# A Strassen MLP inside two attention blocks: two weight groups per step on the way down, operands written after each product, weight differences on GpSimd, and other staging tiles

## The chip, the cores and the metric

The kernel runs on one core of a Trainium2 chip. The time is device microseconds of one execution. Each core has TensorE (PE, matrix products into PSUM), VectorE (DVE), ScalarE (ACT), GpSimd (POOL) and SyncE (SP, whose queue issues all the DMAs here). Matrix products read SBUF and write the eight PSUM banks; DMAs move tiles between DRAM and SBUF.

## The reference

Sixteen sequences of 256 tokens with 512 channels go through two blocks. Block 0 is cross-attention with a mask and a residual, followed by an MLP (layer norm, 512 to 2048 channels, exact gelu, back to 512, residual). Block 1 is self-attention, cross-attention and a small MLP. The change is in the MLP of block 0 (and in what lies just before and after it):

```python
x = x + out
h = layer_norm(x, n2_w, n2_b)
h = jax.nn.gelu(h @ fc1_w + fc1_b, approximate=False) @ fc2_w + fc2_b
return x + h
```

All is float32. Products are made in three passes: an operand is split into a rounded high part and the low rest, and high x high, high x low and low x high are added up in PSUM. A split is one cast on ScalarE (the high part) and one subtract (the low part).

## The kernel before

The tokens are worked in groups of 512 (two sequences), eight groups in all. The kernel has three parts in time: phase 1 (attention of block 0, a stream of heads into which projections are woven), the MLP of block 0 (`Mlp0`), and block 1. TensorE's instructions run in the order in which the program writes them (`manual_schedule`). The instructions of the other engines and of SP are put in order by the framework, by its own estimate of when each is due; each engine then runs its list in order, so an instruction that waits holds up all those behind it. Tiles come from pools; a tile with one buffer can be filled again only when the last reader of its former content is done.

`Mlp0` uses one level of Strassen's scheme in Winograd's form: a product of two 2x2 block matrices takes seven block products instead of eight, from operands that are blocks, sums and differences of blocks (`differences` makes four of them: s1 = a21 + a22, s2 = s1 - a11, s3 = a11 - a21, s4 = a12 - s2). `OPS` says which operand of the tokens and which of the weights belongs to each product.

*The weights.* They are cut into eight groups of 256 hidden channels. `weigh(way, m)` loads a raw group (512 KB, tile `wst`), makes four differences (two on GpSimd, L821 and L822, two on VectorE, L823 and L824) and splits seven blocks into the tiles `w_h` and `w_l` (`split_lazy`, L141 on ScalarE and L142 on VectorE). Way 1 is fc1, way 2 is fc2, which is put into the same tiles when the way up is done with them.

*The way up.* A group of tokens takes four steps of two weight groups each (`up`, 84 products of 128x256 a step). Its seven operands lie in the slots `x_t` and `c_t`, split from the transposed normalized tokens; those of the next group are written (`operand_up`) in the last step, each after the product that last reads its slot. `turn` transposes a tile of 128 tokens (L843) for the next group, with four evictions by ScalarE for even tiles and by VectorE for odd ones (L847). The tile `ho` collects a step's hidden values, which go to DRAM (`hid`, 1 MB a step).

*The way down.* A group of tokens takes eight steps of one weight group each, 42 products a step. For each step the hidden values are loaded (`hidden`, 512 KB, two steps ahead), the sums made (`sums_down`, L789 and L790 on GpSimd, L791 and L792 on VectorE) and seven operands split into one of two sets of slots, both one step ahead:

```python
            for n in range(total):
                ...
                if n + 1 < total:
                    self.sums_down(n + 1)
                    self.operands_down(n + 1)
                ...
                for i in (1, 6, 2, 7, 5, 4, 3):
                    if n or i not in (1, 6):
                        self.product_down(n, i)
                    if m == self.NM - 1:
                        self.end(g, i, xs[g])
```

The seven products of a group (L991) add up over its steps in seven PSUM banks. In the last step `end` adds each of them to the residual tile `x`: seven sums that read PSUM on VectorE (L1021 to L1036) and four on GpSimd (L1022, L1023, L1028, L1029). A product of the next group can start in its bank when those sums have read it. `residual` loads the four tiles of x and adds the bias on GpSimd (L1004).

*The edges.* The end of phase 1 (`last`) splits the first two weight groups, normalizes, turns and writes the first group's operands between the last heads; the other six groups are split in `run`, ahead of its first step. In the last group of the way up, `weigh(2, ...)` follows the steps that free its tiles. At the end `front` loads and transposes the first tokens of block 1 between the last products.

Of the kernel before, what the change touches and what calls it, by code (L numbers as in the profile page):

```python
# [41 lines left out]
def kernel(ctx: ExitStack, tc: tile.TileContext, a, out):  # L42
# [96 lines left out]
    def split_lazy(src, h, l):  # L139

        nc.scalar.copy(h, src)  # L141
        nc.vector.tensor_tensor(l, src, h.bitcast(F32), ALU.subtract)  # L142
# [87 lines left out]
    def ln_stats(pool, src):  # L230

        st = pool.tile([P, nc.vector.BN_STATS_DIM], F32, tag="bnst", name="st")
        mv = pool.tile([P, nc.vector.BN_AGGR_DIM], F32, tag="bnmv", name="mv", bufs=4)
        nc.vector.bn_stats(st, src)
        nc.vector.bn_aggr(mv, st)
        rstd = pool.tile([P, 2], F32, tag="bnrs", name="rstd", bufs=4)
        nc.vector.tensor_scalar(rstd[:, 0:1], mv[:, 1:2], EPS, None, ALU.add)  # L237
        nc.gpsimd.tensor_tensor(out=rstd[:, 1:2], in0=rstd[:, 0:1], in1=nhalf, op=ALU.pow)  # L238
        return mv[:, 0:1], rstd[:, 1:2]

    def normalize(pool, dst, src):
        mean, rstd = ln_stats(pool, src)
# [308 lines left out]
    def phase1():  # L551
# [173 lines left out]
        def last():  # L725
            yield from more_values(NG - 1)
            right.close()
            mlp = w["mlp"] = Mlp0()
            yield from residual(NG - 2, 1)
            for m in range(mlp.EARLY):  # L730
                mlp.weigh(1, m)
                yield 12 * PASS
            yield from residual(NG - 1, 0)
            for t in range(G):
                yield mlp.turn(0, t, mlp.normal(0, t, pool, "xr"))
            mlp.sums()
            for i in range(mlp.NP):
                mlp.operand_up(i)
# [10 lines left out]
    class Mlp0:  # L749
# [13 lines left out]
        NP = 7  # L763
        EARLY = 2
# [5 lines left out]
        def __init__(self):  # L770
# [5 lines left out]
            self.w, self.wp, self.raw, self.banks = {}, {}, {}, {}  # L776

            tiles = pair(self.ins, "x_t") + pair(self.ins, "c_t")
            self.slots = [t[:, i, :] for t in tiles for i in range(KC)]
# [3 lines left out]
            ]  # L783


        def differences(self, a21, a22, a11, a12, out):

            s1, s2, s3, s4 = out
            nc.gpsimd.tensor_tensor(out=s1, in0=a21, in1=a22, op=ALU.add)  # L789
            nc.gpsimd.tensor_tensor(out=s3, in0=a11, in1=a21, op=ALU.subtract)  # L790
            nc.vector.tensor_tensor(s2, s1, a11, ALU.subtract)  # L791
            nc.vector.tensor_tensor(s4, a12, s2, ALU.subtract)  # L792

        def weigh(self, way, m):


            raw = self.pool.tile([P, 4 * 2 * P], F32, tag="wst", name="raw", bufs=3)
            if way == 1:
                src = a["fc1_w"][:, ts(m, 2 * P)].rearrange("(k p) c -> p k c", p=P)
                view = raw.rearrange("p (k c) -> p k c", k=KC)  # L800
                nc.sync.dma_start(out=view, in_=src)
                b = [[view[:, 2 * k : 2 * k + 2, ts(n, P)] for n in range(2)] for k in range(2)]
            else:
                src = a["fc2_w"][ts(m, 2 * P), :].rearrange("(k p) c -> p k c", p=P)
                view = raw.rearrange("p (k c) -> p k c", k=2)
                nc.sync.dma_start(out=view, in_=src)
                b = [[view[:, k, ts(n, 2 * P)] for n in range(2)] for k in range(2)]
            if m not in self.w or way == 2:
                if way == 1:
                    self.wp[m] = sbuf(self.stack, f"w{m}", 1, "right")  # L810
                self.w[m] = tuple(
                    self.wp[m].tile([P, self.NP, 2 * P], F32R, tag=f"w{x}", name=f"w{m}_{x}")
                    for x in "hl"
                )
            diff = self.pool.tile([P, 4, 2 * P], F32, tag="wst", name="diff", bufs=3)

            def like(x):
                return x.rearrange("p (k c) -> p k c", k=2) if way == 1 else x

            t1, t2, t3, t4 = (like(diff[:, i, :]) for i in range(4))  # L820
            nc.gpsimd.tensor_tensor(out=t1, in0=b[0][1], in1=b[0][0], op=ALU.subtract)  # L821
            nc.gpsimd.tensor_tensor(out=t3, in0=b[1][1], in1=b[0][1], op=ALU.subtract)  # L822
            nc.vector.tensor_tensor(t2, b[1][1], t1, ALU.subtract)  # L823
            nc.vector.tensor_tensor(t4, b[1][0], t2, ALU.subtract)  # L824
            h, l = self.w[m]
            for i, x in enumerate((b[0][0], b[1][0], b[1][1])):
                split_lazy(x, like(h[:, i, :]), like(l[:, i, :]))
            split_lazy(diff, h[:, 3:, :], l[:, 3:, :])


        def normal(self, g, t, pool, tag="xn"):
            x = pool.tile([P, C], F32, tag=tag, name="xn")
            nc.sync.dma_start(out=x, in_=xd[0][g][ts(t, P), :])
            normalize(pool, x, x)
            return x

        def turn(self, g, t, x):
# [6 lines left out]
            for c in range(KC):  # L844
                to, gain, offset = self.x[:, c, ts(t, P)], n2[:, 0, c : c + 1], n2[:, 1, c : c + 1]
                if t % 2:
# [5 lines left out]
        def sums(self):  # L852
# [5 lines left out]
            self.differences(b[1][0], b[1][1], b[0][0], b[0][1], [s[:, i] for i in range(4)])  # L858
            self.a = [b[0][0], b[0][1], b[1][1]] + [s[:, i] for i in range(4)]

        def up_slots(self, i):
            return [
                self.slots[8 * x + i].rearrange("p (k n) -> p k n", n=self.W) for x in range(2)
            ]

        def operand_up(self, i):
            split_lazy(self.a[i], *self.up_slots(i))

        def product_up(self, n, i, tag, first):
            g, s = divmod(n, self.NS)  # L870
            ao, bo = self.OPS[i]
            x = self.up_slots(ao)
# [15 lines left out]
            if s == self.NS - 1 and g + 1 < NG:  # L888
# [576 lines left out]
```

## Time and profile before

| what | us |
|---|---|
| median of three runs (2858.71 to 2864.98) | 2864.82 |
| the profiled execution | 2866.24 |
| its span, first to last instruction | 2864.5 |
| TensorE busy | 2700.0 (94%) |
| VectorE busy | 2087.5 (73%) |
| ScalarE busy | 1855.6 (65%) |
| GpSimd busy | 894.9 (31%) |
| first and last product of the way up | 725.8, 1081.1 |
| first and last product of the way down | 1073.8, 1479.0 |

A row of a timeline has the start, the length, the engine, the line, the operation, what it writes and reads, and in brackets how long the engine had been idle before it and who ended that. A row of the waits has who waited for whom, the microseconds in total, how often, and the longest. The TensorE's mean granted clock is 0.974 of full speed.

### The profile page before, as it was taken

How to read it: one execution, taken by the hardware profiler on the slowest of the kernel's cores; microseconds unless marked ns; L12 is line 12 of the kernel's file. 1: busy time of each engine (PE TensorE's matmuls, PEld its weight loads, DVE VectorE, ACT ScalarE, POOL GpSimd, SP SyncE). 2: the span in 40 equal slices, each digit the busy share in tenths (PEclk: the TensorE clock that was granted, in tenths of full speed). 3: DMA queues.
4: the chain of work that ended last, by engine and by line, in shares of the span. 5: the costliest groups of instructions: out<-in, count | busy, mean ns of one | idle time of the engine just before them, and what ended most of it. 6: DMA issues, size and time to landing. Idle time of an engine off the chain costs nothing.

```text
span 2864.5 us, 57571 instructions
## 1 busy us (share of the span) xinstructions
PE 2700.0 (94%) x18970; PEld 2270.2 (79%) x18970; DVE 2087.5 (73%) x6129; ACT 1855.6 (65%) x5504; POOL 894.9 (31%) x960
## 2 busy tenths in 40 slices
PE   7999999997999997898989999999999999999998
PEld 5777777775899986898978777777777777777787
DVE  6676666757865678898977777777777677776887
ACT  4877777777554554444437777777777777787632
POOL 6122221212210115555441222224433233233533
PEclk9999999998999998999999999999999999999999
DMA  7566565554333353434355565566665555555321
GB/s 226 171 195 179 170 179 168 185 169 127 133 130 118 122 183 121 143 124 143 123 191 190 182 189 178 182 186 210 205 192 174 178 181 179 171 177 170 97 100 59
DMA packets 292282, 465.47 MB, mean 162 GB/s; under 512 B 36753, under 2 KB 188817, under 8 KB 287889
## 3 DMA queue, kind: packets, MB, share of 16 engines
q1 hardware_dynamic: 291984, 461.79, 51.2%
q8 instruction: 153, 2.51, 0.4%
q14 instruction: 145, 1.18, 0.1%
HBM read 284.97 MB, written 176.69 MB: 161 GB/s over the span
## 4 chain that ended last, share of the span: by engine, by line
PE 70%; DVE 11%; DMA 9%; ACT 5%; issue 3%; SPq 1%; POOL 1%; POOLq 0%; DVEq 0%; ACTq 0%
PE ps_v L259 15%; PE ps_p L259 14%; PE down L991 10%; PE ps_pt L450 8%; PE ps_z L466 5%; PE ps_s L409 5%; PE up_sc L880 4%; PE up_pt L880 3%; DMA d<-qk 3%; PE up_mm L880 3%; ACT e L434 2%; PE ps_t L278 2%; DMA x<-xd 2%; DVE e L424 1%; DVE c_t L142 1%
## 5 line engine op out<-in xcount | busy, mean ns | idle before, releaser
L434 ACT ACTIVATE e<-e,mn 128x256 f32<-128x256 f32 (+1 forms) x1024 | 487.7, 480 | 86.6 <-DVE mn L424 85.5
L453 ACT COPY pt<-ps_pt 128x512 f32<-128x512 f32 (+1 forms) x768 | 421.4, 554 | 142.0 <-PE ps_pt L450 135.0
L450 PE MATMUL ps_pt<-ident,e 128*128 128x128 f32 x2816 | 439.5, 275 | 13.5 <-ACT pt L453 12.8
L450 PEld LDWEIGHTS ps_pt<-ident,e 128*128 128x128 f32 x2816 | 338.2, 141 | 56.5 <-ACT pt L453 20.0
L409 PE MATMUL ps_s<-stack 97*128 97x256 f32 (+1 forms) x1536 | 334.5, 299 | 28.8 <-ACT e L434 22.0
L409 PEld LDWEIGHTS ps_s<-stack 97*128 97x128 f32 (+1 forms) x1536 | 268.9, 191 | 93.7 <-ACT e L434 39.1
L434 ACT ACTIVATE e<-ps_s,mn 128x256 f32<-128x256 f32 x512 | 244.4, 496 | 65.6 <-DVE mn L420 60.2
L1219 POOL TENSOR_TENSOR x<-x,zz 128x256 f32<-128x256 f32 x128 | 95.2, 744 | 609.7 <-DVE zz L1212 577.3
L238 POOL TENSOR_TENSOR rstd<-rstd,nhalf 128x1 f32<-128x1 f32 x192 | 127.3, 669 | 484.1 <-DVE rstd L237 436.9
L424 DVE CUSTOM_DVE_ANT_0 e<-mb,ps_s 128x256 f32<-128x256 bf16 x512 | 192.6, 415 | 77.9 <-PE ps_s L409 75.2
L991 PE MATMUL down<-w_h,x_t 128*128 128x256 f32 x896 | 187.2, 301 | 55.9 <-DVE x L1032 28.5
L259 PE MATMUL ps_p<-x_t,q_h 128*128 128x512 f32 x640 | 216.1, 419 | 3.6 <-DVE qk L128 3.2
L420 DVE TENSOR_REDUCE mn<-ps_s 128x2 f32<-128x512 f32 x256 | 174.4, 682 | 57.6 <-PE ps_s L409 55.4
L466 PE MATMUL ps_z<-pt,v 128*32 128x256 f32 (+1 forms) x3072 | 205.1, 372 | 5.8 <-ACT pt L453 3.7
L991 PEld LDWEIGHTS down<-w_h,x_t 128*128 128x128 f32 x896 | 155.4, 207 | 61.2 <-issue 34.2
L434 ACT ACTIVATION_READ_ACCUMULATOR e<-e,mn 128x1 f32 x1024 | 197.8, 193 | 0.0
L424 DVE CUSTOM_DVE_ANT_0 e<-tri,ps_s 128x128 f32<-128x128 f32 (+1 forms) x512 | 158.1, 346 | 50.8 <-PE ps_s L409 46.3
L991 PE MATMUL down<-w_h,c_t 128*128 128x256 f32 x896 | 170.2, 286 | 0.0
L466 PEld LDWEIGHTS ps_z<-pt,v 128*32 128x32 f32 x3072 | 84.4, 110 | 106.9 <-issue 27.5
L259 PE MATMUL ps_v<-v_h,c_t 128*128 128x512 f32 x384 | 158.8, 422 | 0.0
L991 PEld LDWEIGHTS down<-w_h,c_t 128*128 128x128 f32 x896 | 145.3, 196 | 0.0
L141 ACT CAST x_t<-sums 128x256 fp32r<-128x256 f32 (+1 forms) x160 | 67.0, 446 | 106.3 <-PE down L991 50.4
(231 smaller groups left out, 7804.9 us busy)
## 6 DMA issues: line engine op xcount, KB each, us to landing
stack<-d SPq DMA_DIRECT2D x1152, 128.0 KB
d<-qk SPq DMA_DIRECT2D x192, 512.0 KB
hid<-ho SPq DMA_DIRECT2D x32, 1024.0 KB
x<-xd SPq DMA_DIRECT2D x128, 256.0 KB
h<-hid SPq DMA_DIRECT2D x64, 512.0 KB
xd<-x SPq DMA_DIRECT2D x96, 256.0 KB
xin<-in_x_dram SPq DMA_DIRECT2D x32, 256.0 KB
xin<-in_ctx_dram SPq DMA_DIRECT2D x32, 256.0 KB
```

The costliest lines, as they stand in the source:

```text
L238: nc.gpsimd.tensor_tensor(out=rstd[:, 1:2], in0=rstd[:, 0:1], in1=nhalf, op=ALU.pow)
L259: nc.tensor.matmul(ps, w[p], x[q], start=(k == 0 and i == 0), stop=(k == kc - 1 and i == 2))
L409: nc.tensor.matmul(ps[:, t, :], u.st[: self.rows, 0, j, ts(t, P)], u.st[: self.rows, 1, j, :], start=True, stop=True,)
L420: nc.vector.tensor_reduce(mn, ps, AX.X, ALU.min)
L424: nc.vector.tensor_tensor_reduce(out=e[:, at], in0=bias[t], in1=ps[:, t, : job.width[t]], scale=-SC, scalar=BIG, op0=ALU.add, op1=ALU.min, ...
L434: nc.scalar.activation(e[:, at], ps[:, t, :] if bias is None else e[:, at], AF.Exp, bias=mn[:, t : t + 1], scale=-1.0, accum_out=u.rs[:, t ...
L450: nc.tensor.transpose(pp[:, ts(x, P)], e[:, at : at + P], ident)
L453: nc.scalar.copy(pt[:, :n], pp[:, :n])
L466: nc.tensor.matmul(z[ts(j, D), w[0] * P :], job.v[u.i * NT + mc][:, u.c * P + j * D : u.c * P + (j + 1) * D], u.pt[j][:, x0 * P : (x0 + le ...
L880: nc.tensor.matmul(ps[:, mm, :], w[p][:, k, :], x[q][:, k, :], start=(first and mm == k == j == 0), stop=(k == 1 and j == 2), skip_group_c ...
L991: nc.tensor.matmul(ps[:, t, :], x[p][:, ts(t, P)], w[q][:, bo, :], start=(m == t == j == 0), stop=(m == self.NM - 1 and j == 2), skip_grou ...
L1219: nc.gpsimd.tensor_tensor(out=xv, in0=xv, in1=zz, op=ALU.add)
```

## The change

The way down works two weight groups in a step: 32 steps of 84 products instead of 64 of 42, with casts, subtracts and sums of 128x512 instead of 128x256, and loads of 1 MB instead of 512 KB. There is one set of slots (512 wide, high and low part each); an operand of the next step is written (`write`) after the product that reads its slot. The weights of a step's two groups are loaded together (`fetch`) into tiles that serve other uses at other times: `raw`, `x0` and `x1` of the pool `px`. All four weight differences are made on GpSimd. Two of the three raw blocks are split in one instruction. Up to the first step of the way up, the low parts of the first two weight groups, the sums and the low parts of the seven operands are made on GpSimd (`early`), and the four normalizations are issued ahead of the weights (`begin`); groups 2 to 7 are split between the first steps. `turn` uses ScalarE alone from the second group on. The residual has one tile instead of two. The operands of the very last step go to places of their own (`late`), so that block 1 can use the slots, and the first query weights of block 1 are loaded in the last group instead of the second. Cut to its core:

```diff
-    def split_lazy(src, h, l):
+    def split_lazy(src, h, l, own):
 
         nc.scalar.copy(h, src)
-        nc.vector.tensor_tensor(l, src, h.bitcast(F32), ALU.subtract)
+        own.tensor_tensor(out=l, in0=src, in1=h.bitcast(F32), op=ALU.subtract)
...
-            nc.gpsimd.tensor_tensor(out=s1, in0=a21, in1=a22, op=ALU.add)
-            nc.gpsimd.tensor_tensor(out=s3, in0=a11, in1=a21, op=ALU.subtract)
-            nc.vector.tensor_tensor(s2, s1, a11, ALU.subtract)
-            nc.vector.tensor_tensor(s4, a12, s2, ALU.subtract)
+            pool.tensor_tensor(out=s1, in0=a21, in1=a22, op=ALU.add)
+            own.tensor_tensor(out=s2, in0=s1, in1=a11, op=ALU.subtract)
+            pool.tensor_tensor(out=s3, in0=a11, in1=a21, op=ALU.subtract)
+            own.tensor_tensor(out=s4, in0=a12, in1=s2, op=ALU.subtract)
...
+        def raw_tile(self, tag):
+            pool = self.pool if tag == "raw" else self.px
+            return pool.tile([P, 4 * N], F32, tag=tag, name="raw")
...
-            nc.gpsimd.tensor_tensor(out=t1, in0=b[0][1], in1=b[0][0], op=ALU.subtract)
-            nc.gpsimd.tensor_tensor(out=t3, in0=b[1][1], in1=b[0][1], op=ALU.subtract)
-            nc.vector.tensor_tensor(t2, b[1][1], t1, ALU.subtract)
-            nc.vector.tensor_tensor(t4, b[1][0], t2, ALU.subtract)
+            pool.tensor_tensor(out=t1, in0=b[0][1], in1=b[0][0], op=ALU.subtract)
+            pool.tensor_tensor(out=t2, in0=b[1][1], in1=t1, op=ALU.subtract)
+            pool.tensor_tensor(out=t3, in0=b[1][1], in1=b[0][1], op=ALU.subtract)
+            pool.tensor_tensor(out=t4, in0=b[1][0], in1=t2, op=ALU.subtract)
             h, l = self.w[m]
-            for i, x in enumerate((b[0][0], b[1][0], b[1][1])):
-                split_lazy(x, like(h[:, i, :]), like(l[:, i, :]))
-            split_lazy(diff, h[:, 3:, :], l[:, 3:, :])
+            for x, at in ((b[0][0], 0), (b2, slice(1, 3))):
+                split_lazy(x, like(h[:, at]), like(l[:, at]), nc.gpsimd if early else nc.vector)
+            split_lazy(diff, h[:, 3:], l[:, 3:], nc.gpsimd if early else nc.vector)
...
         def hidden(self, n):
...
+            h = self.raw_tile("x0" if n % 2 else "raw").rearrange("p (m c n) -> p m c n", m=2, c=2)
+            nc.sync.dma_start(out=h.rearrange("p m c n -> p (m c n)"), in_=self.hid[g][q])
...
         def product_down(self, n, i):
...
+            for mm in range(2):
+                w = self.w[2 * pair + mm]
+                for t in range(2):
+                    for j, (p, r) in enumerate(((0, 0), (0, 1), (1, 0))):
...
         def residual(self, g):
-            x = self.px.tile([P, G, C], F32, tag=f"x{g % 2}", name="x")
+            x = self.px.tile([P, G, C], F32, tag="x1", name="x")
...
+        def begin(self):
+            self.fetch(1, 0, self.raw_tile("raw"))
+            xn = self.px.tile([P, G, C], F32, tag="x2", name="xn")
+            for t in range(G):
+                self.normal(0, t, xn[:, t, :])
+                yield 0.0
+            for m in range(2):
+                self.weigh(1, m, True)
+                yield 12 * PASS
+            for t in range(G):
+                yield self.turn(0, t, xn[:, t, :])
+            self.sums(True)
+            for i in range(7):
+                self.write(i, nc.gpsimd)
+            self.fetch(1, 1, self.raw_tile("x1"))
...
         def run(self, early, after_up):
...
+                if g == NG - 1:
+                    if s == 0:
+                        self.fetch(2, 0, self.raw_tile("x0"))
+                        self.fetch(2, 1, self.raw_tile("x1"))
+                        self.hidden(0)
+                    else:
+                        self.weigh(2, 2 * s - 2)
+                        self.weigh(2, 2 * s - 1)
+                        if s < 3:
+                            self.fetch(2, s + 1, self.raw_tile(f"x{s - 1}"))
+            self.at = self.next
+            self.up(last + 1, [lambda: self.product_down(0, 1), lambda: self.product_down(0, 6)])
...
         def down(self, early, after_up):
...
+            self.hidden(1)
+            for n in range(last + 1):
+                g, q = divmod(n, self.NS)
+                if n == last - 1:
+                    for m in (2, 3):
+                        self.wp[m][0].close()
+                    load = early()
...
+                if q == 0:
+                    xs[g] = self.residual(g)
+                if n + 1 <= last:
+                    self.sums_down(n + 1)
+                    self.next = self.slots
+                    if n + 1 == last:
+                        self.next = [(x, s[1]) for x, s in zip(late, self.slots)]
+                if n + 2 <= last:
+                    self.hidden(n + 2)
                 for i in (1, 6, 2, 7, 5, 4, 3):
                     if n or i not in (1, 6):
                         self.product_down(n, i)
+                    if n < last:
+                        self.write(self.OPS[i][0])
+                    if q == self.NS - 1:
+                        self.end(g, i, xs[g])
```

In the changed kernel the sums of `differences` are lines 786 to 789, `end` has lines 1033 to 1050 (L1046 is the former L1032), the residual's adds are L1018, and a product of the way up or down is L899 or L1005. In the last group of the way down the second pair of weight groups comes first.

## The prediction

> **What bounds the kernel now.** I read the profile in this order: the page's busy table, the table of 20-us windows from 600 to 1560 us (the whole MLP), the waits of TensorE in it, then the timelines around the gaps. First four windows (PE, PEld, DVE, ACT, POOL busy with counts, clock, DMA share, GB/s):
>
> ```profile
> 800.00:820.00 20.00, 20.00 (x170) 20.00 (x169) 15.10 (x31) 11.74 (x24) 4.85 (x5) 1.00 0.34 132
> ...
> 1100.00:1120.00 20.00, 11.34 (x79) 11.35 (x80) 15.38 (x26) 6.01 (x17) 11.31 (x10) 0.68 0.19 63
> ...
> 1160.00:1180.00 20.00, 20.00 (x169) 20.00 (x168) 18.40 (x36) 9.50 (x28) 11.11 (x12) 1.00 0.28 95
> 1180.00:1200.00 20.00, 14.98 (x110) 14.45 (x109) 19.30 (x34) 7.59 (x20) 12.11 (x12) 0.87 0.39 140
> ```
>
> A full window holds 169 matmuls, 0.12 us each. The way up is full from 780 to 1040. On the way down every group of 336 matmuls should take 40.3 us and takes 47.6 (its gaps start at 1240.3, 1288.0 and 1335.7): 7.3 lost, seven times. The four windows from 1040 to 1120 hold 154, 98, 92 and 79: 253 short of 676, 30 us. Two waits name most of the rest:
>
> ```profile
> PE down L991 <- DVE x L1032: 28.5, 7, 5.4
> ```
> ```profile
> PE ps_t L843 <- DVE xn L243: 12.8, 4, 5.2
> ```
>
> The first is the seven group ends, the second the entry into the MLP (692 to 709 us). The timeline of one group end, TensorE, then VectorE, then GpSimd:
>
> ```profile
> 1192.71 0.28 PE L991 MATMUL down<-w_h,x_t 128*128 128x256 f32 x1
> 1196.82 0.55 PE L991 MATMUL down<-w_h,x_t 128*128 128x256 f32 x1 [3.83 <-DVE x L1032]
> ```
> ```profile
> 1177.09 0.42 DVE L142 TENSOR_TENSOR x_t<-h,x_t 128x256 fp32r<-128x256 f32 x1
> 1177.43 0.42 DVE L142 TENSOR_TENSOR x_t<-sums,x_t 128x256 fp32r<-128x256 f32 x1
> ...
> 1191.22 0.67 DVE L1027 TENSOR_TENSOR u<-u,down 128x512 f32<-128x512 f32 x1
> 1191.82 0.68 DVE L1031 TENSOR_TENSOR x<-x,down 128x512 f32<-128x512 f32 x1
> 1192.41 1.12 DVE L142 TENSOR_TENSOR c_t<-h,c_t 128x256 fp32r<-128x256 f32 x1
> 1193.46 1.48 DVE L142 TENSOR_TENSOR c_t<-sums,c_t 128x256 fp32r<-128x256 f32 x1
> ...
> 1196.00 0.68 DVE L1032 TENSOR_TENSOR x<-x,down 128x512 f32<-128x512 f32 x1
> ```
> ```profile
> 1191.97 1.28 POOL L1028 TENSOR_TENSOR x<-x,u 128x512 f32<-128x512 f32 x1 [2.23 <-DVE u L1027]
> 1193.21 1.44 POOL L1029 TENSOR_TENSOR x<-x,u 128x512 f32<-128x512 f32 x1
> ```
>
> TensorE waits for a PSUM bank that L1032 must read. L1032 stands behind two L142 that took 1.12 and 1.48 instead of 0.42, each ending just after a GpSimd instruction: two SBUF inputs on VectorE and a GpSimd instruction take turns, while a sum with PSUM (L1031, 0.68) runs beside it. After the gap matmuls start 0.215 apart for 4.8 us. Spacing when nothing interferes: VectorE 0.335 (128x256) and 0.60 (128x512); GpSimd 0.69 (L789 in the timeline) and 1.24 (L1028 to L1029); ScalarE casts 0.31 and 0.51.
>
> **Way down, steady.** Per group, before: VectorE 8 x 9 x 0.335 = 24.1, GpSimd 16 x 0.69 + 8 x 1.25 = 21.0, together 45.1 us of work that takes turns, against 40.3 of TensorE. After: 36 x 0.60 = 21.6 and 8 x 1.24 + 8 x 1.25 = 19.9, together 41.5; ScalarE falls from 17.4 to 14.3. The larger effect is the deadline. Seven products share seven fixed banks, so the group-end sums of product i must end before product i of the next group starts: 6/7 of a step, 4.3 us in a step of 5.0, 8.6 in a step of 10.1. Walk the last step from its start at 0 in the new VectorE order: product 5 ends at 7.2; GpSimd's adds follow L1041 at 8.0 and end near 9.5 and 11; the new L1046 (old L1032) runs by 10 to 12, product 5 of the next group starts at 15.8; the last bank (4) is read by 13 and wanted at 17.3. The new wait, each operand write behind its own product, has the same 8.6 us and needs one cast (0.6) and one subtract (0.6 to 1.9). A middle step needs 9 x 0.60 + 2 x 1.24 = 7.9 of 10.1. The hidden load becomes 1 MB in 10 us (104 GB/s, with residual and output 157); windows of before move up to 233. The residual's single tile makes loads wait for the stores, queued on SP ahead of one hidden load, which has 10 us of room; its four GpSimd adds are needed 30 us later. So the 7 x 7.3 = 51 us go, of which I give back 2 for the first-layer query weights (4 GpSimd instructions, 5 us) now in the last group: **-49** (bounds -53 and, if half of each end stays, -26).
>
> Here the page "TensorE: Matmul & The Clock Gate", Part 1, would count differently: half rate until about 3.4 us of busy time, so a removed gap of 4.1 returns about 1.7 more, 5.8 per group and 41 in all. The row shows 4.8 us at half rate and 7.3 lost, and I use the row.
>
> **Turn from up to down (30 lost now).** From step 31's start at 0: weight groups 4 and 5 are free at 5.8; casts 2 x 1.8 and subtracts 2 x 2.07 beside the step's own sums end near 11. Only then is tile x0 free, so SP issues hidden(1), and behind it in SP's queue the store of step 30, whose tile the new sums need. 512 KB loads of before took 3.8 to 4.6 us from issue to use (1069.5 to 1073.3); 2 MB at 230 GB/s plus 2 us end at 21 to 22. Then GpSimd 1.25, s2 and two more VectorE places, cast, subtract: product 6 starts near 25.8 instead of 14.4. That is 11.4, plus 3 of slow clock, 1.5 for product 4 behind L955, 3 in the next step, 1 elsewhere: 20. Before, eight residual adds in a row (11.25 us at 1097) made the worst gap; they now come three and one. The differences moved to GpSimd cost 2 x (0.69 - 0.335) = 0.7 of shared time per weight group, 5.7 here, inside those splits. **-10** (bounds: store lands in time, 8 lost, -22; splits late twice, 32 lost, +2).
>
> The page "Perfetto Trace Analysis", section "Optimizing Scalar/DVE Operations", speaks against these edits: VectorE and GpSimd share a read port, so moving work between them might not help. By that rule alone this part gains nothing, and the total would lie 10 higher.
>
> **Entry (40 lost from 640 to 780, 13 of it the second wait).** All four normalizations are now issued before the weights, so the 12.8 and its slow clock (about 4) go, as do most of the 6 missing in 740 to 780, because only two groups are split before step 0 instead of eight queued. Against it GpSimd takes the splits of groups 0 and 1, sums and all seven writes: 8 x 0.69 + 8.7 + 5 + 7 x 1.25 = 28 us in a stretch of some 37, and the attention's 0.4-us rb copies stand behind up to 8 us of it where units last 5. I charge 10: **-13** (bounds -22, +8).
>
> **Small ones.** The odd transposes' four evictions go from VectorE to ScalarE (4 x 0.34, ScalarE is 10 of 20 busy): covered, but one z bank serves them; if the cover goes, up to 14; I take **+4** (0 to +14). The last step's operands are written to other places and the next block's first x goes into x0, free only as that step starts: three us of DMA against 1.4: **+2** (0 to +6). Later instructions have the same TensorE order.
>
> **Sum.** -49 - 10 - 13 + 4 + 2 = -66 against the profiled execution's 2866.2 (span 2864.5 and 1.7 around it; the median of the runs is 2864.8): 2800.
>
> **Rivals.** *Shared port becomes the bound (slower):* with means that VectorE and GpSimd show together in the up stage (L142 128x512 0.81, L789 1.755) a step needs 9 x 0.81 + 2 x 1.755 = 10.8, a group 4 x 10.8 + 8 x 1.44 = 54.7, 7.1 more than now; 8 x 7.1 - 23 of the other parts is +34: 2900. It decides from (47.6 - 11.5)/4 = 9.0 us a step. For it: VectorE is busy 18 to 19 of 20. Against: those means hold the wait for the other, so adding counts it twice, and before runs x169 in mid-group. *Half of each group end stays*, because L1046 still waits for GpSimd: 2866 - 26 - 10 - 13 + 6 = 2823. *The edges eat it*: GpSimd delays attention by 15 at the entry and the turn loses 20 more: 2866 - 49 + 15 + 20 + 6 = 2858. That the change doesn't do what it says is excluded by the built order: writes do alternate with products.
>
> **Numbers.** Likeliest 0.68 (2800; its own range 2772 to 2828), half 0.17, edges 0.05, port 0.10. Faster 0.68 + 0.17 = 0.85, same 0.05, slower 0.10; 0.3% is 8.6 us, about what a measurement of this kernel can tell from no change. The range runs from 2770 (all bounds good but one) to 2845, past the half case with a late entry, leaving out port, edges and a little more.
>
> **What would show it.** Right: windows of the way down at x169 throughout, group period near 40.3, no wait on L1046; one gap near 11 us just before product 6 at the turn, with GpSimd's sums waiting for a DMA; no wait on xn. Wrong: group period over 44, GpSimd and VectorE both filled, rb waits in the attention's tail, or a gap at the turn over 25.

## The result, and the profile after

| | median us (lowest to highest) | ratio to before (95% interval) | down-group period, us |
|---|---|---|---|
| before | 2861.54 (2857.35 to 2864.98) | 1 | 47.90 |
| after | 2844.08 (2838.12 to 2853.9) | 0.9943 (0.9919 to 0.9968) | 47.39 |
| forecast | 2800 | 0.977 | 40.3 |

The change makes the kernel faster by 0.6%, against 2.3% forecast. The profiled execution of after took 2842.86 us with a span of 2841.0; before had 2866.24 and 2864.5. The period is the mean of six groups of the way down, from the last product of the first group to that of the seventh; it is read from one profile each. The two profiles lie 23.4 us apart, the medians 17.5; the parts below add up to the former.

TensorE does the same products in the same order, so its marks show where the difference arises. Offset means after minus before at the same product.

| part | forecast | measured | offset after it |
|---|---|---|---|
| entry, to the first product of the way up | -13 | -15.0 | -15.0 |
| evictions on the way up | +4 | +1.0 | -14.0 |
| turn, to the last product of the first down group | -10 | -8.4 | -22.4 |
| group ends, to the last product of the seventh group | -49 | **-3.1** | -25.5 |
| last group and its edge | +2 | +4.4 | -21.1 |
| the rest of block 1 | 0 | -2.4 | -23.5 |

The forecast's -49 counts seven group ends; in the trace the seventh lies in the row below it. One term failed. Two windows show it (columns as there: PE, PEld, DVE, ACT, POOL busy with counts, clock, DMA share, GB/s):

```profile
1100.00:1120.00 20.00, 20.00 (x169) 20.00 (x168) 17.48 (x20) 8.88 (x15) 9.61 (x8) 1.00 0.23 83
1180.00:1200.00 20.00, 15.68 (x109) 15.27 (x109) 12.55 (x14) 5.57 (x10) 11.23 (x8) 0.83 0.46 157
```

The window with 79 matmuls from 1100 to 1120 is full now; what is left of the turn lies earlier, in gaps of 9.0 us at 1057.57 and 4.7 at 1081.78. But a window like the last one comes back in every group: 109 matmuls, clock 0.83, VectorE idle for 7.4 of 20 us. TensorE's waits from 1100 to 1440 no longer name the sum at the group's end (now L1046). They name operands:

```profile
PE down L1005 <- DVE c_t L142: 19.4, 8, 2.8
PE down L1005 <- ACT x_t L141: 9.3, 7, 2.2
```

Those operands come from s2 on VectorE (L787), which waits for s1 on GpSimd (L786), and GpSimd waits for a load of the residual (L1018 is its bias add). The waits of VectorE and of GpSimd in the same stretch:

```profile
DVE sums L787 <- POOL sums L786: 49.9, 14, 6.8
```
```profile
POOL x L1018 <- DMA x<-xd: 53.3, 7, 8.5
```

The timeline of one group (the last product of the group before it ran at 1165.39): SyncE's queue, GpSimd, VectorE, TensorE.

```profile
1171.22 2.27 SPq L1052 DMA_DIRECT2D xd<-x  x4
1178.94 3.01 SPq L1017 DMA_DIRECT2D x<-xd  x4
```
```profile
1182.79 2.54 POOL L1018 TENSOR_TENSOR x<-x,b_fc 128x512 f32<-128x512 f32 x2 [7.86 <-DMA x<-xd]
1185.28 1.29 POOL L786 TENSOR_TENSOR sums<-raw 128x512 f32<-128x512 f32 x1
1186.54 1.29 POOL L788 TENSOR_TENSOR sums<-raw 128x512 f32<-128x512 f32 x1
1187.78 3.40 POOL L1018 TENSOR_TENSOR x<-x,b_fc 128x512 f32<-128x512 f32 x2
```
```profile
1186.61 1.75 DVE L787 TENSOR_TENSOR sums<-sums,raw 128x512 f32<-128x512 f32 x1 [6.20 <-POOL sums L786]
1188.29 1.75 DVE L142 TENSOR_TENSOR c_t<-raw,x_t 128x512 fp32r<-128x512 f32 x1
1189.97 1.75 DVE L789 TENSOR_TENSOR sums<-raw,sums 128x512 f32<-128x512 f32 x1
```
```profile
1189.13 0.38 PE L1005 MATMUL down<-w_h,x_t 128*128 128x256 f32 x1 [1.57 <-ACT x_t L141]
1192.38 0.58 PE L1005 MATMUL down<-w_h,c_t 128*128 128x256 f32 x1 [2.75 <-DVE c_t L142]
```

The four steps of a group are counted from 0. The order of GpSimd's list is: two residual adds, the sums of step 2, two residual adds. The first add stands still for 7.86 us until the residual has landed; its load leaves SyncE behind the stores of the group before, which empty the same tile. The sums of step 2, which need none of that, stand behind it. They run at 1185.28, TensorE wants the operands at 1187.4, and GpSimd's work beside it stretches VectorE's part (1.75 an instruction instead of 0.68). TensorE loses 1.85 and 3.03 us in two gaps and 24 matmuls at 0.215 after them.

### The profile page after: what moved, and what is told of

The parts are those of the page before. It is cut to its first block, busy times and chain, and to the rows that moved or that the text cites. A ratio compares the mean times of both kernels' runs of the same rounds, so it can differ in the third digit from the quotient of the medians.

```text
span 2841.0 us, 56513 instructions
## 1 busy us (share of the span) xinstructions
PE 2687.6 (95%) x18970; PEld 2263.3 (80%) x18970; DVE 2013.1 (71%) x5722; ACT 1840.9 (65%) x5320; POOL 932.9 (33%) x943
## 4 chain that ended last, share of the span: by engine, by line
PE 65%; DMA 11%; DVE 11%; ACT 5%; issue 4%; POOL 2%; SPq 1%; POOLq 0%; ACTq 0%; DVEq 0%
PE ps_v L259 15%; PE ps_p L259 14%; PE ps_pt L450 8%; PE down L1005 6%; PE ps_z L466 5%; PE ps_s L409 4%; PE up_sc L899 4%; DMA x<-xd 3%; PE up_pt L899 3%; ACT e L434 3%; PE up_mm L899 2%; DMA d<-qk 2%; DMA xd<-x 2%; PE ps_t L278 2%; DVE c_t L142 1%
## 5 line engine op out<-in xcount | busy, mean ns | idle before, releaser
L1005 PE MATMUL down<-w_h,c_t 128*128 128x256 f32 x900 | 265.2, 295 | 24.3 <-DVE c_t L142 24.1
L1005 PE MATMUL down<-w_h,x_t 128*128 128x256 f32 x868 | 254.9, 294 | 18.8 <-ACT x_t L141 18.8
L1005 PE MATMUL down<-w_l,x_t 128*128 128x256 f32 x868 | 253.6, 292 | 0.0
L141 ACT CAST x_t<-sums 128x512 fp32r<-128x512 f32 x156 | 93.5, 620 | 178.0 <-DVE sums L787 121.9
L1005 PEld LDWEIGHTS down<-w_h,c_t 128*128 128x128 f32 x900 | 181.9, 202 | 27.8 <-DVE c_t L142 27.8
L1005 PEld LDWEIGHTS down<-w_h,x_t 128*128 128x128 f32 x868 | 175.3, 202 | 20.6 <-ACT x_t L141 20.6
L1005 PEld LDWEIGHTS down<-w_l,x_t 128*128 128x128 f32 x868 | 175.2, 202 | 0.0
```

What stands on the lines that cost most here:

```text
L1005: nc.tensor.matmul(ps[:, t, :], x[p][:, mm, ts(t, P)], w[r][:, bo, :], start=(q == mm == t == j == 0), stop=(q == self.NS - 1 and mm == 1 ...
```

## Experiments

Theory A: GpSimd's order is the cause (sums behind a waiting add). Rival B: the period is set by the work for which VectorE and GpSimd take turns, and the order only decides where the loss shows.

| run | us | ratio to before (95%) | period |
|---|---|---|---|
| e1_small_adds | 2803.31 | 0.9807 (0.9788 to 0.9826) | 41.96 |
| e2_adds_behind_sums | 2807.76 | 0.9827 (0.9812 to 0.9841) | 42.65 |
| e3_store_first | 2840.04 | 0.9934 (0.9919 to 0.9949) | 47.17 |
| e4_fronts_later | 2843.80 | 0.9944 (0.9928 to 0.9961) | 47.32 |
| e5_bank_read | 2803.60 | 0.9816 (0.9792 to 0.9841) | 42.08 |
| e6_all_orders | 2797.53 | 0.9795 (0.9773 to 0.9817) | 42.11 |
| e7_diffs_vector | 2846.56 | 0.9965 (0.9952 to 0.9978) | 47.39 |
| e8_before_bank_read | 2849.35 | 0.9972 (0.9959 to 0.9986) | 46.78 |
| e9_before_one_tile | 2852.33 | 0.9981 (0.9966 to 0.9997) | 47.44 |
| e10_entry_vector | 2843.77 | 0.9949 (0.9931 to 0.9967) | 47.70 |
| e11_split_adds | 2801.80 | 0.9798 (0.9773 to 0.9822) | 42.11 |
| e12_before_small_adds | 2840.14 | 0.9939 (0.9917 to 0.9960) | 46.86 |

### e1_small_adds: the adds almost without work, in their place

```diff
-                    out=x[:, t, :], in0=x[:, t, :], in1=self.b_fc2, op=ALU.add
+                    out=x[:, t, :1], in0=x[:, t, :1], in1=self.b_fc2[:, :1], op=ALU.add
```

> The four residual adds of each group (L1018, 2.5 and 3.4 us a pair on GpSimd) handle one column of 512 instead of all, so most of the fc2 bias is left out of the result; the place of the adds in GpSimd's queue and their wait for the residual load stay. Theory A (GpSimd's queue: the next step's sums L786 stand behind the waiting add): GpSimd still idles about 8 us in each group in front of L1018 and L786 of step 2 still starts only after the load landed, but 2.5 us earlier than now (the two adds ahead of it are gone), so the 5.0 us of gaps in a group fall to about 2.5, the group period from 47.6 to about 44.5, the time by some 20 us to about 2822. Rival B (the time that VectorE and GpSimd take turns is the bound): 6 us of GpSimd work in 47.6 go whatever waits, the gaps close, the period falls to about 41.5, the time to about 2800.

Measured: 2803.31, period 41.96, which is B's number, not A's. GpSimd's timeline in the same place of a group (the group before it ended at 1155.60):

```profile
1174.12 0.19 POOL L1018 TENSOR_TENSOR x<-x,b_fc 128x1 f32<-128x1 f32 x1 [8.12 <-DMA x<-xd]
1174.75 0.19 POOL L1018 TENSOR_TENSOR x<-x,b_fc 128x1 f32<-128x1 f32 x1 [0.44 <-DMA x<-xd]
1174.89 1.29 POOL L786 TENSOR_TENSOR sums<-raw 128x512 f32<-128x512 f32 x1
```

The wait is as long as before, and it does no harm. The load lands later in the group than in after, so the sums begin at 19.3 us into the group instead of 19.9, hardly earlier. What is shorter is VectorE's part behind them: from the start of L787 to the end of the first operand made from a sum (`c_t<-sums`, on which the longer gap waits) it takes 5.71 us in after and 3.21 here. L787 itself stays at 1.76, beside L788, but L789 and that operand's write take 0.70, and the write of another operand, which stood ahead of L789 in VectorE's list, stands behind it. So the wait alone is not the price, and A's size was wrong: the price is the late start together with the slow chain behind it. This run does not tell A from B.

### e2_adds_behind_sums: the same work in another order

```diff
-            pool.tensor_tensor(out=s3, in0=a11, in1=a21, op=ALU.subtract)
+            self.after = pool.tensor_tensor(out=s3, in0=a11, in1=a21, op=ALU.subtract)
...
+        def bias(self, x, tiles):
+            with tc.issue_after(self.after.ins):
+                for t in tiles:
+                    nc.gpsimd.tensor_tensor(
+                        out=x[:, t, :], in0=x[:, t, :], in1=self.b_fc2, op=ALU.add
+                    )
...
+                self.bias(xs[g], {1: (0, 1, 2, 3)}.get(q, ()))
```

The adds go from `residual` to `bias`, which is called in step 1, behind the sums made there for step 2. In after the program has all four adds ahead of the sums of step 1, and GpSimd's list has them around those of step 2: the framework orders that list itself. So the order is forced by an explicit edge (`issue_after`).

> Same work as the changed kernel on every engine; only the four residual adds of a group stand behind the sums of the group's step 2 in GpSimd's queue instead of two ahead of them and two behind. Theory A: L786 of step 2 no longer waits for the residual load, both gaps of a group (2.0 and 3.0 us, with the slow clock 7) close, period 40.3 to 42, seven to eight groups give 40 to 50 us: 2795 to 2805. Rival B: the amount of work that VectorE and GpSimd must take turns for is unchanged, so the period stays at 47 to 48 and the time at 2844 within 9; the gaps only move.

Measured: 2807.76, period 42.65. B predicted 2844, so B falls. The same instructions in another order take 4.7 us out of each group, and 4 out of the first one, which the table counts to the turn (its gap of 4.7 us becomes 1.5). GpSimd's timeline and part of VectorE's, in a group that follows one ended at 1157.46:

```profile
1174.50 1.62 POOL L786 TENSOR_TENSOR sums<-raw 128x512 f32<-128x512 f32 x1 [5.03 <-DVE c_t L142]
1176.08 1.29 POOL L788 TENSOR_TENSOR sums<-raw 128x512 f32<-128x512 f32 x1
1177.33 6.86 POOL L1023 TENSOR_TENSOR x<-x,b_fc 128x512 f32<-128x512 f32 x4
```
```profile
1176.16 1.77 DVE L787 TENSOR_TENSOR sums<-sums,raw 128x512 f32<-128x512 f32 x1 [1.19 <-POOL sums L786]
1177.96 1.67 DVE L789 TENSOR_TENSOR sums<-raw,sums 128x512 f32<-128x512 f32 x1
```

The sums now run 17.0 us into the group and wait only for their own tile; the adds come when the residual has landed, and wait for nothing. VectorE's part is stretched here as in after. The first operand from a sum is ready 26.9 us into the group in after, 23.8 in e1 and 23.9 in e2: e1 has the shorter chain, e2 the earlier start. One thing besides GpSimd's order changed in e2 as in e1: the framework also put L789 ahead of the write of another operand in VectorE's list. Of the 3.1 us that e2's operand is earlier, 2.5 are the earlier start of L787 and 0.5 the chain behind it; no run changes one list alone. What is left is a wait of TensorE at the group's end for the sum of product 5 (L1050 is L1046 of after), which after, whose groups stand still earlier, did not show:

```profile
PE down L1005 <- DVE x L1050: 9.5, 6, 1.8
```

### e5_bank_read: that sum without GpSimd

```diff
-                add(block(1, 1), block(1, 1), p[g, 5], ALU.add)
+                v = self.flat("v")
+                add(v, self.u2, p[g, 5], ALU.add)
+                nc.gpsimd.tensor_tensor(out=block(1, 1), in0=block(1, 1), in1=v, op=ALU.add)
```

and GpSimd's add of u2 to block (1,1) under product 7 goes; all on top of e2.

> On top of the version with the adds behind the sums: the sum of product 5 with the block (1,1) no longer waits for GpSimd. VectorE adds u2 and the bank into a tile of its own, and GpSimd adds that to the block (as many instructions as now on each engine). In the version before it TensorE waited for this sum (L1050 there) six times, 9.5 us in all, with a gap of 2.0 us in each group. If what holds the bank is the wait for GpSimd's earlier add, the gaps go and the period falls from 42.9 to 41 or less: some 12 to 15 us, about 2794. If the bank is held because VectorE comes to that place late in its own queue (operand writes at 1.4 to 1.8 us beside GpSimd), the wait moves to the new sum and the period stays at 42.9: 2808 within 4.

Measured: 2803.60, period 42.08. The gaps at the group's end are gone, but only 0.57 us a group comes of it, 4 in all as in the medians, a third of what was expected; the intervals of e2 and e5 overlap. TensorE's waits from 1100 to 1400 are then

```profile
PE down L1005 <- DVE c_t L142: 4.1, 7, 0.6
PE down L1005 <- ACT x_t L141: 3.5, 6, 0.6
```

two gaps of 0.9 us in each group's step 1, a dozen microseconds behind the group's end, and 42.08 stays instead of 40.3.

### e6_all_orders and e11_split_adds: all orders together

e6 is e5, with e3's and e4's edits, and with the differences of the last two weight groups and the splits of block 1's query weights behind the sums on GpSimd. In e11 two of the four adds go behind the sums of step 3.

> Everything that is only order, together: adds behind the sums, the bank of product 5 read without GpSimd, the store of step 30 ahead of the load hidden(1), the differences of the last two weight groups and the splits of the first-layer query weights behind the sums on GpSimd, the last step's transposes behind products 7, 5, 4 and 3. If each wait is one of queue order, the gains add: 36 (adds) + 13 (bank) + 4 (turn) + 5 to 8 (end, where the gap had grown to 9.7 us) = 58 to 61 below 2844: 2783 to 2786. If VectorE and GpSimd are short of time as such, what is freed in one place comes back in another and the time stays above 2798.

> The version with all orders together, but two of the four residual adds behind the sums of step 2 and two behind those of step 3. It had 2.0 us a group left over 40.3, in two gaps of 0.9 that wait for operand writes of step 1, right behind the group end. If these come from too much shared work in one step (L1023, 6.9 us beside VectorE at 1.77 an instruction), spreading it takes up to 1 us a group: about 2791. If they come from the group end's own VectorE work, nothing changes: 2797 within 4.

Measured: 2797.53 and 2801.80. e6 is 2.05% faster than before and has the lowest median; its interval overlaps those of e1, e5 and e11. It differs from after by order, and by the sum of e5. It misses its expectation by 12 to 15 us: by the medians the bank brought 4 instead of 13, and all that e6 has beyond e5 6 instead of 9 to 12. In e11 the same two gaps stay with two of the adds moved a step on, so the 1.8 us a group that are left don't come from four adds in one step. From where they come is open. VectorE is not full there: it is busy for 17.6 of the 20 us from 1160 to 1180 in e5. Two things in e5's rows point at its list. The sums of step 1 (L786 at 1159.98) start just after the last operand write that reads the former sums (it ends at 1159.85), and that write stands behind the group end's own sums; and behind L787 VectorE's list has, in e5, e6 and e11, the write of another operand ahead of L789, as in step 2 of after. No run tests either.

### e3_store_first: the turn

```diff
+            with tc.issue_after(self.store[last - 1].ins):
                 self.hidden(1)
```

> At the turn from up to down the store of step 30 (its tile is the one that the first sums need) is put ahead of the load hidden(1) in SyncE's queue. If, as the prediction said, the store stands behind a load that waits for tile x0 (issued 1053.9, the store 1054.3, the sums L786 at 1062.8 waiting for it), the store goes out at 1045 to 1048, the sums run among the weight differences at 1053 to 1056, and the gap of 9.0 us ahead of product 6 shrinks to 2 or less; with slow clock 6 to 9 us: 2836 to 2838. If the sums' VectorE part is held by the splits anyway (VectorE and GpSimd taking turns there), the gap stays above 6 and the time within 3 of 2844.

In after, the turn looks as the prediction said, a store behind a load on SyncE, and GpSimd's sums waiting for the store:

```profile
1053.87 0.34 SPq L978 DMA_DIRECT2D raw<-hid  x1
1054.32 0.37 SPq L938 DMA_DIRECT2D hid<-ho  x1
```
```profile
1062.83 1.26 POOL L786 TENSOR_TENSOR sums<-raw 128x512 f32<-128x512 f32 x1 [2.22 <-DMA hid<-ho]
```

Measured: 2840.04, within the noise of after. The store does leave SyncE ahead of the load, but only when the step's last gelu is done (1057.32, the store at 1057.35), before which there is nothing to store. In after that gelu ends at 1053.95 and the store leaves at 1054.32, so the load ahead of it held it up by 0.4 us at most: the order on SyncE was not what made the store late. In e3 the sums then stand behind GpSimd's weight differences in its list and start at 1063.94. The first gap falls from 9.0 to 6.7, the next rises from 4.7 to 5.8. Several things end within a few microseconds of each other here, and moving one brings 1.4 us at the turn in the trace and nothing that the times show.

### e4_fronts_later: the end

```diff
-                    if n == last and i in (1, 6, 7, 4):
-                        after_up((1, 6, 7, 4).index(i))
+                    if n == last and i in (7, 5, 4, 3):
+                        after_up((7, 5, 4, 3).index(i))
```

> In the last step of the way down the four transposes of the next block's first tokens stand behind products 7, 5, 4 and 3 instead of 1, 6, 7 and 4. Their loads go out at 1442.9 when tile x0 is free and landed at 1445.4, 5.4 us after TensorE wanted them. If that load is the whole of the end's loss, the gap of 5.6 us at 1440 falls to 1 or less and the time by 4 to 5 us, to about 2839; if something behind (evictions of the transposes before the next block's first projection) takes it over, the gap goes and the time stays within 2 of 2844.

Measured: 2843.80, unchanged. The gap of 5.6 us at 1440 is gone, and the next wait has grown by 2.5 (3.6 in after); TensorE's waits from 1440 to 1500:

```profile
PE ps_p L259 <- DVE qk L133: 6.1, 1, 6.1
```

The end of the way down is a stretch where block 1's first projections wait anyway. Counted from the end of the seventh group, this trace is some 2.5 us ahead of that of after 1,000 matmuls into block 1, and 5,000 matmuls on nothing is left. Where that is given back wasn't settled. In e6, which has this edit too, the lead over e5 counted in the same way is 2.9 us after 1,000 matmuls and 4.8 at the program's end; what follows the way down takes 1379 to 1390 us in these profiles, so single ones can't decide a few microseconds.

### e7_diffs_vector and e10_entry_vector: the work moved to GpSimd

```diff
-            pool.tensor_tensor(out=t2, in0=b[1][1], in1=t1, op=ALU.subtract)
+            (nc.gpsimd if early else nc.vector).tensor_tensor(out=t2, in0=b[1][1], in1=t1, op=ALU.subtract)
```

(t4 alike) for e7; in e10 `nc.vector` for `nc.gpsimd if early else nc.vector`, and `self.write(i)` for `self.write(i, nc.gpsimd)`.

> The changed kernel with two of the four weight differences of a group back on VectorE (all groups but the first two). The prediction charged 0.7 us of shared time for each weight group, 5.7 us at the turn, inside the splits. If that was right the gap of 9.0 us before product 6 at the turn shrinks by 2 to 6 and the time falls to 2838 to 2842. If the differences lie beside other waits (at the turn the sums L786 wait for a store, not for GpSimd), the time stays at 2844 within 3; if VectorE is the scarcer of the two at the turn, it rises by 3 to 6.

> The changed kernel with the splits of the first two weight groups and the sums and writes of the first tokens on VectorE instead of GpSimd; the normalizations stay ahead of the weights. The prediction put 23 us of gain on the removed wait for normalized tokens and charged 10 us for GpSimd's 28 us of work; measured 15 in the two profiles. If the place of the normalizations makes the gain, it stays within 3: 2841 to 2847. If GpSimd's help is needed because VectorE is full there, the way up starts 5 to 10 us later: 2849 to 2854. If the 10 us of charge were real, it starts 5 to 10 earlier: 2834 to 2839.

Measured: 2846.56 and 2843.77, with intervals that overlap after's (2844.08). Which of the two engines makes these pieces is worth nothing that can be measured. The entry's gain is then not GpSimd's; the wait for normalized tokens, 12.8 us before, is 1.1 in after and 2.0 in e10, which fits the normalizations ahead of the weights. No run separates these from the other change of order there (six of the eight weight groups split later).

The page "Perfetto Trace Analysis" of the Trainium skill says in its section "Optimizing Scalar/DVE Operations" that moving work between VectorE and GpSimd might not help, since they share a read port. Both runs agree with it; the gain of the turn, which the prediction set against it, is not of such a move: from the start of its last up step to the end of the first down group e7 takes 70.4 us and after 70.5, before 78.6.

### e8, e9 and e12: what bound before

e8 puts e5's edit into the kernel before; e9 gives its residual one tile as in the change; e12 is e1 on before.

```diff
-            x = self.px.tile([P, G, C], F32, tag=f"x{g % 2}", name="x")
+            x = self.px.tile([P, G, C], F32, tag="x1", name="x")
```

> The kernel before with one edit: the sum of product 5 with block (1,1) (its L1032) reads the bank into a tile of its own and GpSimd adds that to the block. The prediction read the seven gaps of 4.1 us (7.3 us lost with the slow clock) as this sum standing behind two operand writes and GpSimd's adds. If the wait for GpSimd in it is the cause, the gaps fall to 1 or less and the time to about 2859 - 7 x 6 = 2817; if the two long operand writes ahead of it on VectorE are (1.12 and 1.48 us instead of 0.42), about 1.7 of 4.1 us stays or goes: 2840 to 2850; if the loss moves to the next bank (product 4), nothing changes: 2859 within 4.

> The kernel before with one edit of the change alone: one residual tile (x1) instead of two in turn. In its trace GpSimd already waits 7.8 us in each group for the residual load (L1004, at 1206.3), because SyncE issues that load at 1201.4 behind the stores of the group before; with one tile the load must also wait until those stores have landed, some 2 to 3 us later. If the single tile is what costs the changed kernel its group ends, the sums behind the add come too late here too and the period rises by 2 or more: 2859 + 14 to 35 = 2873 to 2894. If it is the queue order together with the twice larger step (only one step of sums ahead), the sums here still come in time: 2859 within 5.

> The kernel before with its four residual adds of a group on one column of 512 (most of the fc2 bias left out). It takes 5 us of work that VectorE and GpSimd must take turns for out of every group, far (20 us) from the group's end. If before was bound by that shared time (45.1 us a group against a period of 47.6), the period falls by 4 to 5 us and the time to 2825 to 2830. If before was bound at the group end alone (the bank that L1032 must read), nothing changes: 2859 within 4.

e8 measured 2849.35, with a period of 46.78: the sum's wait for GpSimd was a small part of before's gap, 1.1 us a group. The 28.5 us of one wait become three larger waits at the same place, all on VectorE's sums of the group's end:

```profile
PE down L991 <- DVE x L1025: 8.5, 6, 1.5
PE down L991 <- DVE v L1032: 7.5, 7, 1.3
PE down L991 <- DVE u L1021: 4.8, 5, 1.8
```

In e8's trace each of these sums stands behind operand writes of the next step, stretched ones among them (1.50 us ahead of L1025, 1.12 ahead of L1032). So before was late at the group's end because VectorE came to these sums late. Writing the operands product by product does not cure that by itself: in e2 L1050 again stands behind two writes of 1.40 and 1.76 us, and TensorE waits for it. Only with e5's edit on top are these waits gone.

e9 measured 2852.33, no slower than before, so the single tile as such costs nothing there. The load leaves SyncE about 13 us into the group in before and in e9, and 14 in after (12.3 to 13.3, 11.6 to 13.3, 13.5 to 15.2 in six groups each): it is late because it stands behind the stores on SyncE with two tiles too.

e12 measured 2840.14. The period falls by 1.0, the wait on L1032 stays at 28.5, and the turn gets 6.7 shorter (there before had eight of these adds in a row). Taking 5 us of shared work out of a group returns 1 of them, so before was not bound by shared time either.

## Why the prediction was wrong

**The step that failed** is the sentence "The residual's single tile makes loads wait for the stores, queued on SP ahead of one hidden load, which has 10 us of room; its four GpSimd adds are needed 30 us later." It asked when the adds' result is needed. What counts is who stands behind the adds on GpSimd: the sums of step 2, whose operands TensorE wanted 2 us after these sums could start. The chain from there on VectorE is slowed by the very adds. e2 shows it: with the sums ahead of the adds 28 us more come back between the ends of the first and the seventh group ((47.39 - 42.65) x 6) and 4 in the first group. e1 shows that the wait does no harm when the adds are almost no work. So the loss is neither the wait nor the shared time alone, but an operand that comes 3 us too late by both.

The sign stood in the profile of before. Its GpSimd already waits in each group, with the next sums behind:

```profile
1206.33 2.74 POOL L1004 TENSOR_TENSOR x<-x,b_fc 128x512 f32<-128x512 f32 x2 [7.79 <-DMA x<-xd]
1209.02 0.92 POOL L789 TENSOR_TENSOR sums<-h 128x256 f32<-128x256 f32 x1
```

There these sums are for the group's fourth step, which starts 22.4 us into the group: 15.1 of products and 7.3 of the loss at the group's end. The sums ran at 20.8. With the loss at the group's end taken out, that step would have started at 15.1. By this count, which is worked out and was not run, the loss at the group's end covered GpSimd's wait in before, and the change uncovered it.

**The mechanism of the group ends** was half right. In after no wait on L1046 is left; in e2, whose groups no longer stand still in step 2, TensorE waits for the same sum, up to 1.8 us. The walk had it done 10 to 12 us after the last step's start; in e2 it ends at about 17.7 (7.6 into the next group), and product 5 wants the bank at 15.8. e5 takes this wait away. But of 7.3 us a group only 47.90 - 42.08 = 5.8 was had, 41 instead of 51 in seven groups, since no run goes below 41.96. That these are also the 5.8 and 41 of the prediction's other count is chance: in e5 the granted clock is 1.00 from 1110 to 1390, so no slow pace is left there, and what is left are the two gaps of step 1. And e8 shows that GpSimd's adds had a small part in before's gap.

**Turn, -10:** measured -8.4, near by size (the gap ahead of product 6 is 9.0 instead of 11.4, plus 4.7 later), not by the steps told: the store was late by its gelu and not by the load ahead of it (e3), and 3 of the 4.7 us go with the order of the adds (e2). **Entry, -13:** measured -15.0 in the first profile, and 8 to 15 in the later ones of variants with the same entry, so a part of the agreement is luck; the 10 us charged for GpSimd's 28 us were not seen when e10 took that work away. **Evictions, +4:** 1.0, the cover held. **End, +2:** 4.4 for the last group, in which the seventh group end should also have been won; the three microseconds of DMA came on top of a later release of x0 (loads out at 1442.85, TensorE idle from 1440). e4 takes the gap away and the time stays. **Rivals:** shared port as the bound is refuted by e2 and e12 (its sum also left out the +6 of the small terms). The case "half of each group end stays" lies on the right side, but by another way than it named: nearly all stayed, and L1046 had no part in it. Of the signs, "group period over 44" came, and "GpSimd and VectorE both filled" did not. That 2844 still lies inside the range to 2845 is luck: that end stood for half of the group ends with a late entry, and the entry was not late.

## What to carry to other kernels

Before an instruction with a wait is called harmless, list what stands behind it on its in-order engine, and when those are needed; the need for its own result says nothing. When a stall is to be taken out of a loop, look for other engines' waits that end inside it: they are covered now and come next. And an order that is cheap to force (an edge, no new work) was worth more here than the change itself: 36 of the 47 us by which e6's median lies below after's come with the four adds of e2 (33 of 42 by the ratios to before). Whoever forces one list should read the others again, since the framework may order them anew as well.

## What was unexpected of the hardware

A gap of TensorE costs itself, and some gaps also cost the pace after them, for which the granted clock falls to 0.50. Around gaps of 2 to 6 us it does so for 3.41 or 6.83 us at a time (in after from 1190.75 to 1197.58). Matmuls that start 0.12 us apart then start 0.215 apart: 15 to 27 of them (3.4 to 5.9 us) after the gaps of 3.0 in after, 20 to 24 (4.4 to 5.3) after before's of 4.1. The slow pace need not begin with the first matmul: after a gap of 3.04 us in e4 it begins 0.4 us later, after one of 2.05 in e2 1.1 us later, and both times some 16 matmuls are slow. The length of the gap alone does not decide: of e2's five lone gaps of 2.0 one was followed by the slow clock, four (1.98 to 1.99) were not. e2's pair of 1.07 and 1.48 brought it too; lone gaps of 1.5 us and less and the pairs of 0.9 in e5 did not. The first of the two rows has e2's gap of 2.05, the second one of 1.22 (mean clock 0.91 and 1.00):

```profile
1160.00:1180.00 20.00, 18.23 (x140) 18.06 (x139) 18.75 (x22) 5.85 (x11) 11.44 (x8) 0.91 0.58 197
1200.00:1220.00 20.00, 18.56 (x153) 18.18 (x152) 18.78 (x23) 5.71 (x10) 9.47 (x7) 1.00 0.45 144
```

So e2, with a gap of 2.0 left in most groups, gains nearly all: its mean clock from 1170 to 1400 is 1.00, that of after from 1160 to 1440 is 0.93. The page "TensorE: Matmul & The Clock Gate" of the Trainium skill, Part 1, has half rate until about 3.4 us of busy time; the rows agree at their lower end and go up to 5.9.

VectorE's sums and writes from two SBUF tiles take 1.67 to 1.79 us beside GpSimd's sums and adds instead of 0.68, and those adds 1.72 instead of 1.24 (L1023 in e2: 6.86 for four). Yet 5 us a group less of such work in before (e12) was worth 1.0: there a stretched instruction cost next to nothing, while in after, where TensorE waited for the end of the chain, it did.
